# Four column tiles of 32 in place of two of 64 for the 65-column attention products of a four-layer graph-attention stack

## The chip, the core and the metric

The kernel runs on one core of a Trainium2 chip. The metric is the device time of one launch in microseconds. Before the change three runs gave 3209.97, 3210.28 and 3212.03 us; the median, 3210.28 us, is the time to compare with.

## What is computed

The input is `x` of shape (16, 1024, 256) in float32 and one adjacency matrix of 1024 x 1024 integers that all 16 batch entries share. Four graph-attention layers follow one another, each with a layer norm and a ReLU ahead of it and a residual sum behind it:

```
h = relu(layernorm(x));  x = x + L0(h, adj)     # 4 heads of 64
h = relu(layernorm(x));  x = x + L1(h, adj)     # 1 head of 256
h = relu(layernorm(x));  x = x + L2(h, adj)     # queries times keys, 1 head of 256
h = relu(layernorm(x));  x = x + L3(h, adj)     # 4 heads of 64
```

Layers 0, 1 and 3 score a pair of nodes by a leaky ReLU of (source score + target score); layer 2 scores it by a dot product. In each layer the scores are masked by the adjacency matrix, go through a softmax over the neighbours, and weigh a sum over the projected rows:

```
alpha = softmax(where(adj, leaky_relu(s_src[j] + s_dst[i]), -inf), axis=j)
h_out[i] = sum_j alpha[i, j] * Wh[j]
```

All products are in float32.

## The kernel before, in words

The function `fast` does the work; `general`, behind a flag that is found at run time, is a fallback that these inputs do not enter. All of a batch entry's rows (8 tiles of 128 nodes) stay in SBUF through the four layers, and five entries can be on the chip at a time.

The softmax is not normalised until the end. For a layer with a leaky ReLU of a sum the exponential of the score is the larger of two products of a source factor and a target factor; factors that depend on one node alone are pulled out, so that VectorE makes a whole tile of weights with one instruction at L950 (`p = max(row, ke) * mask`, 128 keys by 512 queries). TensorE then multiplies these weights with the values. The values carry one more column, which the product turns into the softmax's denominator: with heads of 64 the moving operand has 65 columns, with one head of 256 it has 257.

The order of all work is written by a planner. Every piece is a step with an engine, a cost in microseconds, a due time and the buffers that it takes and gives back (`plan.add`); `plan.order()` plays the steps through once while the program is built and gives one fixed order. Steps of different layers and different entries lie interleaved on each engine: while layer 0 of one entry runs, layer 3 of another and layers 1 and 2 of others run between its steps.

The names that matter here:

- `product` (L531 to L534) is the helper that all large products go through. It splits the 128 stationary columns into two matmuls of `COLS = 64` columns each, with outputs on PSUM partitions 0 to 63 and 64 to 127[...]. All of these matmuls have line L534.
- `steps_a` makes the weights and the products of layers 0 and 3. For each half of the queries, each head and each tile of keys there is one VectorE step `weigh` (L950) and one TensorE step `attend`: four calls of `product`, one for each 128 queries, into the tile `acc` of PSUM. One layer of one entry has 64 such steps, the kernel has 2048 of them.
- `steps_b` does the same for layers 1 and 2. Its `attend` writes the tile `accb` with 257 columns; its `score` (layer 2) writes `pp` from `qT` and `hT` with 512 columns.
- `prologue` norms and transposes a layer's input (L796: float32 transposes of 128 x 128 into `pp`) and projects it with `product` (`projected`: tiles `pp<-w,hTp` with 268 or 259 columns, `pp<-w2v,hT` with 256; `query`: `pp<-hT,w` with 512). L883 transposes the score factors, with 32 or 8 stationary columns.

A step of `steps_a` as the planner sees it on TensorE:

```
s = plan.add(PE, 0.47, at, attend, (s, last_a[1]), take=("acc",) if jt == 0 else (), give=give)
```

Of the kernel before, what the change touches and what calls it, by code (L numbers as in the profile page):

```python
# [18 lines left out]
P = 128  # L19
# [3 lines left out]
HALF = 512  # L23

COLS = 64

# [462 lines left out]
def fast(  # L491
# [35 lines left out]
    def buf(tag, shape, dtype=F32, name=None):  # L527
        pool = psum if tag in ("pp", "acc", "accb") else sb
        return pool.tile(shape, dtype, name=name or tag, tag=tag, bufs=bufs[tag])

    def product(to, stationary, moving, start, stop):  # L531

        for c in range(0, P, COLS):
            nc.tensor.matmul(  # L534
                to[c : c + COLS],
                stationary[:, c : c + COLS],
                moving,
                start=start,
                stop=stop,
                skip_group_check=True,  # L540
            )
# [17 lines left out]
    def mask_of(half, jt):  # L559
        return mask[half][jt // HT][:, jt % HT, :]  # L560
# [173 lines left out]
    class Layer:  # L734
# [5 lines left out]
        def prologue(self, due, step, stats):  # L740
# [35 lines left out]
            for n, t0 in enumerate(range(0, NT, 2)):  # L776
# [34 lines left out]
                for k in range(2):  # L811
                    t = t0 + k

                    def projected(t=t, t0=t0, k=k):
                        pv = T["pv", t] = buf("pp", [P, HALF])
                        for c in range(KC):
                            product(
                                pv[:, :cols],
                                T["hT", t0][:, c, k * P : (k + 1) * P],
                                w[:, c, :cols],  # L820
                                start=(c == 0),
                                stop=(c == KC - 1),
                            )
# [31 lines left out]
            if not self.gat:  # L855
                for dc in range(KC):
                    for n0 in range(0, N, HALF):

                        def query(dc=dc, n0=n0):
                            pq = T["pq", dc, n0] = buf("pp", [P, HALF])  # L860
                            for c in range(KC):
                                product(
                                    pq,
                                    w12[:, c, dc * P : (dc + 1) * P],
                                    self.hT[:, c, n0 : n0 + HALF],
                                    start=(c == 0),
                                    stop=(c == KC - 1),
                                )

                        s = plan.add(PE, 1.72, at, query, (*copies, *w12_ready), take=("pp",))  # L870

                        def keep(dc=dc, n0=n0):
                            nc.scalar.copy(self.qT[:, dc, n0 : n0 + HALF], T["pq", dc, n0])

                        evicted.append(plan.add(ACT, 0.6, at, keep, (s,), give=("pp",)))
                self.ready = tuple(evicted)
                return
# [61 lines left out]
    def steps_a(lay, due, span):  # L939
        heads = lay.heads  # L940
        d = F // heads
        T = {}
        n = 2 * heads * NT
        for i in range(n):
            half, hd, jt = i // (heads * NT), i // NT % heads, i % NT
            at = due + span * i / n

            def weigh(half=half, hd=hd, jt=jt):
                p = T["p", half, hd, jt] = buf("p", [P, HALF])
                nc.vector.scalar_tensor_tensor(  # L950
                    p, lay.rows[half, hd], lay.ke[:, hd, jt : jt + 1], mask_of(half, jt), op0=OP.max, op1=OP.mult
                )

            s = plan.add(
                DVE, 0.67, at, weigh, (last_a[0], *lay.ready, lay.row_ready[half, hd], *mask_ready[half, jt // HT]),
                take=("p",), give=("row4",) if jt == NT - 1 else (),
            )
            last_a[0] = s

            def attend(half=half, hd=hd, jt=jt):  # L960
                if jt == 0:
                    acc = buf("acc", [P, HALF])
                    T["acc", half, hd] = acc[:, : HT * (d + 1)].rearrange("p (t d) -> p t d", t=HT)
                p = T.pop(("p", half, hd, jt))
                for t in range(HT):
                    product(
                        T["acc", half, hd][:, t, :],
                        p[:, t * P : (t + 1) * P],
                        lay.val[:, jt, hd, :],
                        start=(jt == 0 and t == 0),  # L970
                        stop=(jt == NT - 1),
                    )

            give = ("p", "val4") if i == n - 1 else ("p",)
            s = plan.add(PE, 0.47, at, attend, (s, last_a[1]), take=("acc",) if jt == 0 else (), give=give)
            last_a[1] = s
            if jt != NT - 1:
                continue

            def divide(half=half, hd=hd):  # L980
                if hd == 0:
                    T["o", half] = buf("o", [P, HT, F])
                acc = T.pop(("acc", half, hd))
                rden = small.tile([P, HT, 1], F32, name="rden")
                nc.vector.reciprocal(rden, acc[:, :, d : d + 1])
                nc.vector.tensor_mul(  # L986
                    T["o", half][:, :, hd * d : (hd + 1) * d], acc[:, :, :d], rden.to_broadcast([P, HT, d])
                )

            s = plan.add(DVE, 0.62, at - EARLY, divide, (s,), take=("o",) if hd == 0 else (), give=("acc",))  # L990
            if hd != heads - 1:
                continue
            its = (half * HT, (half + 1) * HT)
            s = lay.elu(T, half, its, at - EARLY, (s,), (4, 2.3, 2.45), ("o",))
            if lay.layer == 3:
                b = lay.b

                def store(its=its, b=b):
                    nc.sync.dma_start(
                        out=out[b].rearrange("(t p) f -> p t f", p=P)[:, its[0] : its[1], :],  # L1000
                        in_=x_tiles[b][:, its[0] : its[1], :],
                    )

                s = plan.add(SP, 0.1, at, store, (s,))
                plan.add(LAND, 3.0, at, lambda: None, (s,), give=("x",) if half else ())
# [284 lines left out]
```

## Time and profile before

| | |
|---|---|
| median of 3 runs | 3210.28 us |
| the profiled execution, its own time | 3207.69 us |
| its span, first to last instruction | 3205.9 us |
| granted TensorE clock, mean | 0.993 |
| TensorE matmul busy | 3101.3 us, 97% |
| TensorE weight loads busy | 2150.1 us, 67% |
| VectorE busy | 2740.2 us, 85% |
| ScalarE busy | 1304.6 us, 41% |
| matmuls recorded | 48774, and as many weight loads |
| DMA | 127.41 MB, 40 GB/s on the mean |

Times of instructions are in nanoseconds or microseconds as marked. "PE" is TensorE's matmul and "PEld" its weight load, which runs beside matmuls. Matmuls are pipelined: an instruction's duration goes from its start to the modelled end of its output, and the next one starts well before that, so the sum of durations is more than the busy time, and the price of a matmul in a stream is the distance from one start to the next. A line "acc<-val,p 128*64 128x65" is a product with stationary `p` (128 rows, 64 columns), moving `val` (128 rows, 65 columns), written to `acc`.

### The profile page before, as it was taken

How to read it: one execution, taken by the hardware profiler on the slowest of the kernel's cores; microseconds unless marked ns; L12 is line 12 of the kernel's file. 1: busy time of each engine (PE TensorE's matmuls, PEld its weight loads, DVE VectorE, ACT ScalarE, POOL GpSimd, SP SyncE). 2: the span in 40 equal slices, each digit the busy share in tenths (PEclk: the TensorE clock that was granted, in tenths of full speed). 3: DMA queues.
4: the chain of work that ended last, by engine and by line, in shares of the span. 5: the costliest groups of instructions: out<-in, count | busy, mean ns of one | idle time of the engine just before them, and what ended most of it. 6: DMA issues, size and time to landing. Idle time of an engine off the chain costs nothing.

```text
span 3205.9 us, 108219 instructions
## 1 busy us (share of the span) xinstructions
PE 3101.3 (97%) x48774; PEld 2150.1 (67%) x48774; DVE 2740.2 (85%) x5584; ACT 1304.6 (41%) x3143; POOL 117.0 (4%) x89
## 2 busy tenths in 40 slices
PE   3799999999999999999999999999999999999996
PEld 2676666767676676766767676676767667675665
DVE  4987689898888989888898888989888898986697
ACT  4334444334344434434334334434434444343421
POOL 0000000000000000000000000000000000000000
PEclk9899999999999999999999999999999999999998
DMA  5101001101011010111101011110101101010011
GB/s 187 55 22 32 22 18 35 48 26 58 24 40 42 25 57 23 45 35 38 45 25 58 25 36 41 35 48 25 58 22 40 43 25 42 25 35 19 24 35 49
DMA packets 85910, 127.41 MB, mean 40 GB/s; under 512 B 8768, under 2 KB 44480, under 8 KB 85440
## 3 DMA queue, kind: packets, MB, share of 16 engines
q1 hardware_dynamic: 81408, 118.06, 11.7%
q8 instruction: 384, 6.29, 0.8%
q10 hardware_dynamic: 4032, 2.36, 0.2%
q14 instruction: 86, 0.70, 0.1%
HBM read 103.02 MB, written 17.37 MB: 38 GB/s over the span
## 4 chain that ended last, share of the span: by engine, by line
PE 92%; DVE 5%; DMA 1%; ACT 1%; issue 0%; ACTq 0%; SPq 0%
PE pp L534 31%; PE acc L534 28%; PE accb L534 27%; PE pp L796 4%; DVE p L950 3%; DMA raw<-in_adj_dram 1%; DMA w<-in_L_gnn_W_dram 0%; DVE p L1020 0%; ACT junk L1121 0%; PE pp L883 0%; DVE o L927 0%; DVE xt L928 0%; DVE bn L728 0%; DVE o L986 0%; ACT mask L656 0%
## 5 line engine op out<-in xcount | busy, mean ns | idle before, releaser
L950 DVE SCALAR_TENSOR_TENSOR p<-row,ke,mask 128x512 f32<-128x512 f32 x2048 | 1428.0, 742 | 100.3 <-PE acc L534 95.6
L534 PEld LDWEIGHTS acc<-val,p 128*64 128x64 f32 x32768 | 1073.7, 138 | 225.9 <-issue 102.6
L534 PE MATMUL acc<-val,p 128*64 128x65 f32 x32768 | 1114.0, 223 | 26.2 <-DVE p L950 26.1
L534 PE MATMUL accb<-val,p 128*64 128x257 f32 x8192 | 934.9, 380 | 0.9 <-ACT o L1085 0.9
L534 PEld LDWEIGHTS accb<-val,p 128*64 128x64 f32 x8192 | 567.2, 136 | 288.3 <-issue 6.6
L534 PE MATMUL pp<-qT,hT 128*64 128x512 f32 x2048 | 480.9, 594 | 0.0
L534 PE MATMUL pp<-w,hTp 128*64 128x268 f32 (+1 forms) x3072 | 399.1, 390 | 1.7 <-ACT hTp L807 1.7
L1047 ACT ACTIVATE u<-pp 128x512 f32<-128x512 f32 x256 | 152.8, 597 | 408.1 <-PE pp L534 361.6
L782 ACT ACTIVATE h<-xt,nshift,rstd 128x256 f32<-128x256 f32 x512 | 277.6, 595 | 80.9 <-DVE nshift L761 77.7
L534 PEld LDWEIGHTS pp<-w,hTp 128*64 128x64 f32 x3072 | 201.2, 138 | 107.7 <-issue 23.7
L534 PEld LDWEIGHTS pp<-qT,hT 128*64 128x64 f32 x2048 | 131.9, 137 | 175.0 <-issue 161.5
L728 DVE BATCH_NORM_STATS2 bn<-xt 128x6 f32<-128x256 f32 x512 | 212.3, 415 | 9.7
L756 POOL TENSOR_TENSOR rstd<-rstd,neg_half 128x8 f32<-128x8 f32 x64 | 114.5, 1789 | 2484.1 <-DVE rstd L753 2135.0
L922 ACT ACTIVATE ex<-o 128x256 f32<-128x256 f32 (+1 forms) x192 | 121.0, 630 | 206.1 <-DVE o L986 202.1
L1085 ACT ACTIVATE o<-accb,rden 128x256 f32<-128x256 f32 x128 | 60.9, 476 | 348.7 <-DVE rden L1079 348.6
L1087 ACT ACTIVATE o<-accb,rdens 128x256 f32<-128x256 f32 x128 | 60.2, 470 | 346.5 <-DVE rdens L1079 346.5
L1052 DVE SCALAR_TENSOR_TENSOR p<-u,p 128x512 f32<-128x512 f32 x256 | 174.4, 681 | 23.6 <-ACT p L1048 23.4
L1020 DVE SCALAR_TENSOR_TENSOR p<-row,ke,mask 128x512 f32<-128x512 f32 x256 | 186.1, 742 | 0.0
L1053 DVE TENSOR_TENSOR p<-p,mask 128x512 f32<-128x512 f32 x256 | 177.1, 692 | 8.8
L837 ACT ACTIVATE val<-pp 128x4 f32<-128x4 f32 (+1 forms) x384 | 67.3, 176 | 284.6 <-PE pp L534 281.4
L927 DVE SCALAR_TENSOR_TENSOR o<-ex,o 128x256 f32<-128x256 f32 (+1 forms) x192 | 131.3, 684 | 52.6 <-ACT ex L923 52.5
L796 PE MATMUL pp<-ident,h 128*128 128x128 f32 x1024 | 166.3, 289 | 9.8 <-ACT h L782 5.3
(75 smaller groups left out, 1823.6 us busy)
## 6 DMA issues: line engine op xcount, KB each, us to landing
row<-er_d SPq DMA_DIRECT2D x288, 256.0 KB, 3.2
xt<-in_x_dram SPq DMA_DIRECT2D x16, 1024.0 KB, 9.4
out_dram<-xt SPq DMA_DIRECT2D x32, 512.0 KB, 3.7
raw<-in_adj_dram SPq DMA_DIRECT2D x32, 256.0 KB, 4.5
w<-in_L_gnn_W_dram ACTq DMA_DIRECT2D x3, 256.0 KB
a_bc<-in_L_gnn_a_dram ACTq DMA_DIRECT2D x6, 128.0 KB, 9.4
wraw<-in_L_gnn_W_dram ACTq DMA_DIRECT2D x2, 256.0 KB
er_d<-er_s SPq DMA_DIRECT2D x32, 16.0 KB, 1.4
```

Source lines behind the costliest of these rows:

```text
L534: nc.tensor.matmul(to[c : c + COLS], stationary[:, c : c + COLS], moving, start=start, stop=stop, skip_group_check=True,)
L728: nc.vector.bn_stats(st, x_tiles[b][:, t, :])
L756: nc.gpsimd.tensor_tensor(T["rstd"], T["rstd"], neg_half, OP.pow)
L782: nc.scalar.activation(h, x_tiles[b][:, t, :], AF.Relu, bias=T["shift"][:, t : t + 1], scale=T["rstd"][:, t : t + 1],)
L796: nc.tensor.transpose(tp[:, c, k * P : (k + 1) * P], T["h", t0 + k][:, c * P : (c + 1) * P], ident)
L922: nc.scalar.activation(T["ex", key], T["o", key], AF.Exp)
L927: nc.vector.scalar_tensor_tensor(o, ex, -1.0, o, op0=OP.mult, op1=OP.max)
L950: nc.vector.scalar_tensor_tensor(p, lay.rows[half, hd], lay.ke[:, hd, jt : jt + 1], mask_of(half, jt), op0=OP.max, op1=OP.mult)
L1020: nc.vector.scalar_tensor_tensor(p, lay.rows[half, 0], lay.ke[:, 0, jt : jt + 1], mask_of(half, jt), op0=OP.max, op1=OP.mult)
L1047: nc.scalar.activation(u, e, AF.Exp, scale=1.0 - SLOPE)
L1052: nc.vector.scalar_tensor_tensor(p, u, 1.0, p, op0=OP.max, op1=OP.mult)
L1053: nc.vector.tensor_mul(p, p, mask_of(half, jt))
```

## The change

The helper gets a parameter for the width of a column tile, and the products of `steps_a` (layers 0 and 3) are made with 32 columns a tile. All other products keep 64.

```diff
+NARROW = 32
...
-    def product(to, stationary, moving, start, stop):
+    def product(to, stationary, moving, start, stop, cols=COLS):
 
-        for c in range(0, P, COLS):
+        for c in range(0, P, cols):
             nc.tensor.matmul(
-                to[c : c + COLS],
-                stationary[:, c : c + COLS],
+                to[c : c + cols],
+                stationary[:, c : c + cols],
                 moving,
                 start=start,
                 stop=stop,
...
                         lay.val[:, jt, hd, :],
                         start=(jt == 0 and t == 0),
                         stop=(jt == NT - 1),
+                        cols=NARROW,
                     )
```

The planner's costs, due times and buffers are as before, so every engine's steps keep their order; on TensorE each run of 65-column matmuls has twice as many of them, each with a stationary operand of 32 columns, and nothing is added, removed or moved on any other engine or queue.

## The prediction

> **What bounds the kernel now.** I read the page first: busy shares, then the chain that ended last.
>
> ```profile
> PE 3101.3 (97%) x48774; PEld 2150.1 (67%) x48774; DVE 2740.2 (85%) x5584; ACT 1304.6 (41%) x3143; POOL 117.0 (4%) x89
> PE 92%; DVE 5%; DMA 1%; ACT 1%; issue 0%; ACTq 0%; SPq 0%
> PE pp L534 31%; PE acc L534 28%; PE accb L534 27%; PE pp L796 4%; DVE p L950 3%; DMA raw<-in_adj_dram 1%; DMA w<-in_L_gnn_W_dram 0%; DVE p L1020 0%; ACT junk L1121 0%; PE pp L883 0%; DVE o L927 0%; DVE xt L928 0%; DVE bn L728 0%; DVE o L986 0%; ACT mask L656 0%
> ```
>
> TensorE's matmul queue makes 92% of the chain, and the tile that the change touches, `acc`, 28%. A busy share is a mean, so next the busy times in a stretch from the middle, where one batch entry goes in and one comes out every 190.7 us:
>
> ```profile
> 1190.70:1381.40 190.70, 190.70 (x3045) 132.63 (x3043) 169.96 (x345) 79.77 (x192) 7.34 (x5) 1.00 0.13 38
> ```
>
> The columns are length, PE, PEld, DVE, ACT, POOL, granted clock, DMA. PE is busy for all 190.70 us, DVE for 169.96. No wait is left on TensorE there that could absorb or give back anything: what a matmul costs in its stream is what the kernel costs. Last, the groups of the touched tile by form, and the timeline of PE alone (start us, length us, line, tile, count):
>
> ```profile
> L534 PE MATMUL acc<-val,p 128*64 128x65 f32 x32768 | 1114.0, 223 | 26.2 <-DVE p L950 26.1
> L534 PEld LDWEIGHTS acc<-val,p 128*64 128x64 f32 x32768 | 1073.7, 138 | 225.9 <-issue 102.6 <-DVE p L950 39.0 <-DVE o L927 7.5
> ```
>
> ```profile
> 1506.06 0.66 PE L796 MATMUL pp<-ident,h 128*128 128x128 f32 x4
> 1506.65 0.69 PE L534 MATMUL acc<-val,p 128*64 128x65 f32 x16
> 1507.16 1.07 PE L534 MATMUL pp<-w,hTp 128*64 128x268 f32 x8
> 1508.07 0.64 PE L534 MATMUL acc<-val,p 128*64 128x65 f32 x16
> 1508.53 1.05 PE L534 MATMUL pp<-w,hTp 128*64 128x259 f32 x8
> ...
> 1511.22 0.64 PE L534 MATMUL acc<-val,p 128*64 128x65 f32 x16
> 1511.79 0.66 PE L796 MATMUL pp<-ident,h 128*128 128x128 f32 x4
> ```
>
> ```profile
> 1528.29 2.97 PE L534 MATMUL acc<-val,p 128*64 128x65 f32 x96
> 1531.09 3.65 PE L534 MATMUL accb<-val,p 128*64 128x257 f32 x32
> 1534.57 2.50 PE L534 MATMUL acc<-val,p 128*64 128x65 f32 x80
> ```
>
> Take distances from start to start. 96 matmuls of 65 columns last 2.80 us (1528.29 to 1531.09): 29.2 ns each, although one has a length of 223. The two column tiles run side by side, so the unit is a pair: 48 pairs, 58.3 ns. A pair of 257 columns takes 3.48/16 = 217.5 ns; 512 columns (1484.34 to 1486.06 us, 8 matmuls) take 430. From 257 to 512 that is 0.83 ns a column. The pair is thus set by the stream of moving columns: the array is full already, and four tiles side by side stream no less than two.
>
> The second thing to see is what a change of tile width costs. Between `acc` and `pp<-w,hTp`, both 64 wide, nothing: 16 matmuls take 8 x 58.3 = 466 ns, and 1508.07 to 1508.53 is 0.46. Into the 128-wide transposes the same 16 take 0.57 (1511.22 to 1511.79), 0.10 us more. Out of them, the 16 take 0.51 (1506.65 to 1507.16), 0.05 more; and eight transposes take 1.02 (1546.30 to 1547.32) where four take 0.59, so that one is 0.108 and 0.16 is left over for going in and out. So a switch costs 0.10 us in which nothing is started, and 0.05 us in which the first weights are waited for: 0.15 us.
>
> [...]
>
> **The change part by part.** Planner and other engines keep their order; 16,384 products become 32,768, with two weight loads and two matmuls each in the records: `acc` goes from 32,768 matmuls to 65,536, in the same places.
>
> 1. The stream. 16,384 pairs (16,384 x 58.3 ns = 955 us) become 16,384 groups of four. If the four tiles run side by side, a group lasts what its moving columns last. By the line above 65 columns would be 217.5 - 192 x 0.833 = 57.6 ns; from 256 columns (`pp<-w2v,hT`, 1548.77 to 1552.32 us less 0.10 for the transposes behind: 215.6) it is 56.5. [...] I take 56.7: 16,384 x 1.6 = **-27 us**. Bounds: 0, and -43 (a slope of 0.84 ns, 55.7 ns).
> 2. New width switches. In the built program's order, `acc` follows a 64-wide product directly 525 times and is followed by one 597 times (the rest of its neighbours are transposes, where the width switched before). All 1122 cost nothing now and become switches between 64 and 32. From 32 to 64: 0.10 + 0.05, and the tiles of a group start one after the other: of a pair, two last 0.28 us together where one lasts 0.27 (the first two at 1514.91), some 7 ns apart, so the fourth starts about 13 ns later than the second did: 597 x 0.164 = **+98 us**. From 64 to 32: 0.10, and half of the 0.05, since half the columns are loaded: 525 x 0.125 = **+66 us**. The trace shows no such switch; below, 0.11 and 0.151 (+148 us together), above, 0.151 and 0.18 (+187). That a drain gives time back is excluded, since PE has no wait to save.
> 3. Switches that exist already: 188 from full width into `acc` lose about 26 ns of load, 116 out of it gain 13 ns: **-3 us**.
> 4. Instruction supply: twice as many instructions for `acc`, 64 in place of 32 a step of 467 ns. Costed at nothing[...].
> 5. VectorE's `p` and `rden` are hidden under PE in the steady stretch (169.96 of 190.70 us); a slower PE gives them more room, and may save some of the 26 us that `acc` waits for `p` (not counted, lower bound only). No queue, DMA or wait is added.
>
> Sum: -27 + 98 + 66 - 3 = +134. Against the profiled execution 3207.7 + 134 = 3341; the median of the runs shown is 2.6 us above it, so **3344 us**, own range 3300 to 3405.
>
> **The rivals.**
> - *No drain between 64 and 32: faster.* Every switch with a drain in this trace has a transpose on one side. If the drain belongs to the transpose mode and not to the tile's width, step 2 falls away and step 1 stays: 3210 - 27 - 3 = 3180, or 3210 if step 1 is nothing too. For it: the confounding; that 128 to 32 (L796 to L883) shows no drain. [...] It decides as soon as a switch costs under 24 ns (27 us / 1122).
> - *Issue becomes the bound: much slower.* A step now has 32 matmuls. [...] With today's 14.6 ns for each load or matmul it would be 64 x 14.6 = 934: +957. It decides from 7.3 ns an instruction. Against it: the two matmuls of a pair start some 7 ns apart[...]; for it: no stream in the trace goes faster than 14.6.
> - *The four tiles run two at a time:* 955 us twice, 4165. [...] I count it with the one before.
>
> **How the numbers follow.** Drain 0.62, no drain 0.22, issue or half concurrency 0.16. A measurement of this kernel tells about 0.2%, 6 us, from no change. Faster: two thirds of the no-drain case, 0.15. Same: 0.06. Slower: 0.79. The range takes the drain case and the no-drain case, 3178 to 3410; what is left out is the issue case.
>
> **What would show it.** Right: start-to-start 0.46 to 0.57 us or so for a lone step of 32 matmuls of 32 columns between 64-wide products, long runs at 57 to 58 ns a group, PE at 100% in a period of about 199 us, `accb` and `pp` rows unchanged in length but with about 0.15 us lost ahead of each. Wrong: runs of `acc` no longer than the stream between 64-wide products (no drain), or a long run of `acc` at 100 ns a group or more (issue).

## The result, and the profile after

The changed kernel takes 3445.16 us (median of 4 runs, 3443.0 to 3446.68) against 3210.12 us before: 1.0731 times as long, 95% interval 1.0712 to 1.0749, or 235 us more. The profiled execution has a span of 3442.1 us and a mean granted clock of 0.993, as before, so the clock is not the cause. Its busy shares and the chain that ended last, from the page:

```profile
PE 3250.5 (94%) x81542; PEld 2113.0 (61%) x81542; DVE 2753.6 (80%) x5584; ACT 1309.1 (38%) x3143; POOL 116.9 (3%) x89
PE 92%; issue 3%; DVE 2%; DMA 1%; ACT 1%; ACTq 0%; SPq 0%
PE pp L536 31%; PE acc L536 30%; PE accb L536 27%; PE pp L798 4%; DVE p L952 1%; DMA raw<-in_adj_dram 1%; DMA w<-in_L_gnn_W_dram 0%; ACT junk L1124 0%; PE pp L885 0%; DVE o L929 0%; DVE xt L930 0%; DVE bn L730 0%; DVE o L989 0%; ACT ex L925 0%; ACT ex L924 0%
```

The matmul count is as forecast (48774 + 32768). What is new is "issue 3%": some 100 of 3442 us, in which TensorE stood still and waited for nothing that the profile shows. Before it was 0%. A stretch of 206 us from the middle shows it too (length, PE, PEld, DVE, ACT, POOL, clock, DMA):

```profile
1412.00:1618.00 206.00, 200.89 (x5095) 130.11 (x5091) 170.70 (x344) 80.29 (x191) 7.34 (x5) 1.00 0.12 37
```

PE is busy for 200.89 of 206 us, where it was busy without a gap before. (The stretches of 206 us around it have 204.71, 204.40 and 202.04.) The group of the changed tile says the same; the last field is the idle time ahead of it and what ended it:

```profile
L536 PE MATMUL acc<-val,p 128*32 128x65 f32 x65536 | 1113.6, 222 | 103.4 <-issue 80.1 <-DVE p L952 23.0
```

The waits for VectorE's weights are the 23 us that they were. Next the timeline of PE alone, where single steps stand between 64-wide products, and one long run:

```profile
1610.02 0.66 PE L536 MATMUL acc<-val,p 128*32 128x65 f32 x32
1610.61 1.12 PE L536 MATMUL pp<-w,hTp 128*64 128x268 f32 x8
1611.66 0.66 PE L536 MATMUL acc<-val,p 128*32 128x65 f32 x32
1612.25 1.10 PE L536 MATMUL pp<-w,hTp 128*64 128x259 f32 x8
...
1633.40 2.93 PE L536 MATMUL acc<-val,p 128*32 128x65 f32 x192
1636.26 3.70 PE L536 MATMUL accb<-val,p 128*64 128x257 f32 x32
```

A lone step now takes 0.59 us from start to start, 0.46 before, and the 64-wide product behind it 1.05 (1610.61 to 1611.66), 0.91 before. That is the drain on both sides (the time that a change of width costs before the stream runs again), 0.27 us for going in and out with the faster stream already taken off. The run of 192 takes 2.86 us; less 0.14 for the two switches it is 56.7 ns a group of four: 0.14 is the sum of the parts of the two switches that fall into this distance, the wait of the first group behind the switch in (0.024) and the idle time of the switch out (0.113). And one place of another kind, in the middle of a run:

```profile
1692.71 2.36 PE L536 MATMUL acc<-val,p 128*32 128x65 f32 x152
1696.54 0.32 PE L536 MATMUL acc<-val,p 128*32 128x65 f32 x8 [1.47 <-issue]
```

After 152 matmuls TensorE stands idle for 1.47 us and then goes on, without a semaphore. Over the single instructions of this trace there are some 88 such stalls of more than 0.2 us, about 101 us in all; 23 us of them fall in the first 200 us, 57 in the middle, 22 in the last 100. Count all of TensorE's recorded instructions (loads, matmuls and its few semaphore instructions): every stall comes after 193 or 194 of them, modulo 256.

So the 235 us are: new switches +162, the stream -27, existing switches -3, stalls +101, together 233.

### The profile page after: what moved, and what is told of

It is laid out like the page before. It is cut to its first block, busy times and chain, and to the rows that moved or that the text cites. A ratio compares the mean times of both kernels' runs of the same rounds, so it can differ in the third digit from the quotient of the medians.

```text
span 3442.1 us, 173756 instructions
## 1 busy us (share of the span) xinstructions
PE 3250.5 (94%) x81542; PEld 2113.0 (61%) x81542; DVE 2753.6 (80%) x5584; ACT 1309.1 (38%) x3143; POOL 116.9 (3%) x89
## 4 chain that ended last, share of the span: by engine, by line
PE 92%; issue 3%; DVE 2%; DMA 1%; ACT 1%; ACTq 0%; SPq 0%
PE pp L536 31%; PE acc L536 30%; PE accb L536 27%; PE pp L798 4%; DVE p L952 1%; DMA raw<-in_adj_dram 1%; DMA w<-in_L_gnn_W_dram 0%; ACT junk L1124 0%; PE pp L885 0%; DVE o L929 0%; DVE xt L930 0%; DVE bn L730 0%; DVE o L989 0%; ACT ex L925 0%; ACT ex L924 0%
## 5 line engine op out<-in xcount | busy, mean ns | idle before, releaser
L536 PEld LDWEIGHTS acc<-val,p 128*32 128x32 f32 x65536 | 976.9, 110 | 433.8 <-issue 261.2
L536 PE MATMUL acc<-val,p 128*32 128x65 f32 x65536 | 1113.6, 222 | 103.4 <-issue 80.1
L536 PE MATMUL accb<-val,p 128*64 128x257 f32 x8192 | 949.0, 383 | 5.9 <-issue 5.6
L536 PE MATMUL pp<-qT,hT 128*64 128x512 f32 x2048 | 490.6, 602 | 2.4 <-issue 1.4
L536 PE MATMUL pp<-w,hTp 128*64 128x268 f32 (+1 forms) x3072 | 410.7, 397 | 3.5 <-ACT hTp L809 1.7
L1051 ACT ACTIVATE p<-pp,shift_col 128x512 f32<-128x512 f32 x256 | 174.7, 683 | 0.0
```

The source lines that it names most:

```text
L536: nc.tensor.matmul(to[c : c + cols], stationary[:, c : c + cols], moving, start=start, stop=stop, skip_group_check=True,)
L1051: nc.scalar.activation(p, e, AF.Exp, bias=shift_col, scale=SLOPE)
```

## The experiments

Each edit is shown against the changed kernel, unless another is named.

The first theory after the result: the switches cost what was forecast, and the rest is instruction supply. The page counts the DMA packets that carry instructions; those of queue 8, before and after:

```profile
q8 instruction: 384, 6.29, 0.8%
```

```profile
q8 instruction: 640, 10.49, 1.3%
```

The columns are packets, MB and share of the DMA engines. 97,548 recorded loads and matmuls before make 254 a packet, 163,084 after make 255; the 65,536 that came in addition came with exactly 256 packets more, so a packet of 16.4 KB is 256 instructions of 64 bytes. The trace also keeps the time of every single packet, and this ties the stalls to them: each of the changed kernel's 89 idle gaps of more than 20 ns that the profile puts down to issue ends between 1.22 and 1.60 us after a packet has landed, where less than 8% of all its matmuls start. The same holds for all 498 such gaps of the six runs that have any, at 1.19 to 1.61 us; the four other kernels have none. The rival: the switches upset the order of steps, and TensorE waits for VectorE's weights without the profile naming it.

**All products in tiles of 32.** No 64-wide tile is left, hence no switch between 64 and 32.

```diff
-COLS = 64
+COLS = 32
```

> All large products in tiles of 32 columns, so that no 64-wide tile is left and the 1122 new width switches are gone, while the 65-column runs need as many instructions as in the changed kernel (and the wide ones twice as many). In the changed kernel 235 us are lost: by the groups' distances, switches cost +162 and the faster stream gives -27, which leaves some 100 us that the chain of waits calls issue. Theory A, instruction supply: instructions come in blocks of 256 and not faster than one block in about 3.4 us (13.4 ns each), while a run of 32-wide 65-column groups uses one in 7.1 ns; the stalls stay or grow, since the wide products between the runs now use more too: 3210 - 27 - 15 + 100 to 180 = 3270 to 3350 us, with issue at 3% or more of the chain. Rival B, the order of steps no longer fits (waits for VectorE's weights after the switches): without switches nothing is late and the kernel is faster than before, about 3170 us.

Measured: 3392.25 us, 1.0569 (1.0552 to 1.0587). Slower than before without any new switch, so the rival falls; but above the expected range of 3270 to 3350. The chain has

```profile
PE 91%; issue 5%; DVE 2%; DMA 1%; ACT 1%; ACTq 0%; SPq 0%
```

and the single instructions show 194 stalls over 0.2 us, 191 us, nearly twice those of the changed kernel. With -27 for the stream, and -7 for earlier first matmuls after 274 transposes (27 ns each in the changed kernel), the sum is 3367; some 25 us stay unaccounted for.

**The mirror image.** The 65-column products at 64 as before, all wider ones at 32.

```diff
-COLS = 64
+COLS = 32
...
-NARROW = 32
+NARROW = 64
```

> The mirror image: the 65-column products in tiles of 64 as before, all wider ones (256 to 512 columns) in tiles of 32. As many switches between 64 and 32 as in the changed kernel (1124), but no stream that uses an instruction in under 14.6 ns. Theory A: switches alone, 526 x 0.151 + 598 x 0.125 = +154 us, 3355 to 3375 us, issue at 0% of the chain, no idle gap of a microsecond inside a run. Rival B (late VectorE work through the switches): the other 100 us appear here too, about 3465 us.

Measured: 3366.46 us, 1.0484 (1.0467 to 1.0502). As many switches as in the changed kernel, at about the forecast price (+157 us, +154 forecast); the chain has no issue in it:

```profile
PE 92%; DVE 5%; DMA 1%; ACT 1%; issue 0%; ACTq 0%; SPq 0%
```

The two kernels show each part of the change without the other: width switches without stalls cost 157 us, and narrow tiles without new switches 182. They are not the two terms of the sum: in the kernel with all products in tiles of 32 the neighbours are narrow too, and its stalls are 191 us, not 101.

**Wider products at full width.** This asks what the drain belongs to, since before the change every drain had a transpose on one side.

```diff
-COLS = 64
+COLS = 128
...
-NARROW = 32
+NARROW = 64
```

> The 65-column products in tiles of 64 as before, all wider ones at the full width of 128, one matmul a pass. No transpose stands between them, so this asks whether a switch between two plain products of different width drains, without any 32-wide tile. If the width drains: 1122 x 0.151 = +169 us, and the transposes no longer switch against the wide products (246 x 0.15 = -37 us): about 3340 us. If the drain belonged to the transposes: none between the products, 3210 us. Instruction supply plays no part (fewer instructions than before).

Measured: 3367.64 us, 1.0492 (1.0474 to 1.0509). The drain belongs to the width. The timeline of PE shows both halves of it:

```profile
1625.21 0.60 PE L798 MATMUL pp<-ident,h 128*128 128x128 f32 x4
1625.74 1.15 PE L536 MATMUL acc<-val,p 128*64 128x65 f32 x32
1626.83 0.66 PE L798 MATMUL pp<-ident,h 128*128 128x128 f32 x4
1627.41 0.69 PE L536 MATMUL acc<-val,p 128*64 128x65 f32 x16
1628.03 1.99 PE L536 MATMUL pp<-w2v,hT 128*128 128x256 f32 x8
```

16 matmuls of 65 columns between a transpose and a plain 128-wide product take 0.62 us, 0.15 more than their stream of 0.47: now the plain product drains. Four transposes behind such a product, of their own width, take 0.53 (1625.21 to 1625.74); the same four behind 64-wide ones 0.58. It came out 28 us above my 3340, and a switch into 128 costs more than I took: the first two plain 128-wide matmuls behind a switch start 0.105 us later than in their stream, not 0.05, 597 x 0.055 = 33 us.

**TensorE alone.** A kernel of nothing but runs of products, a DVE copy between the stretches. One stretch of it; `cols` is the width of a tile, `wide` the number of moving columns, and the others differ in these and in the length.

```diff
+    for k in range(320):
+        cols, wide = [(32, 65)][k % 1]
+        product(acc, k % 4, cols, wide, k == 0, k == 319, call)
```

> TensorE alone, the graph layers left out (the output is the input copied): runs of products without any wait inside, a block being all 128 stationary columns. 320 blocks of 65 columns in tiles of 64: 58.3 ns a pass, 37.3 us. The same in tiles of 32: theory A (one block of 256 instructions in 3.4 to 3.75 us) 68 to 75 us, after a start at 56.7 ns a pass out of what was fetched ahead; if only the array counted, 36.3 us. 160 blocks of 130 columns in tiles of 32: 13.9 ns an instruction, at the limit, 35.5 to 37.5 us. 80 blocks of 257 columns in tiles of 64, of 32, of 128: 34.7 us each. 80 blocks of 257 alternating 64 and 32: 79 switches x 0.14 = +11 us, 46 us; alternating 128 and 64, and 128 and 32: the same +11 us each if the width drains, nothing if only transposes do.

The timeline of PE, where no semaphore can stop a stretch:

```profile
123.35 37.55 PE L37 MATMUL a64x<-v,p 128*64 128x65 f32 x1280 [0.44 <-DVE v L46]
...
172.60 3.83 PE L37 MATMUL b32x<-v,p 128*32 128x65 f32 x254 [0.53 <-DVE v L62]
177.43 2.02 PE L37 MATMUL b32x<-v,p 128*32 128x65 f32 x128 [1.01 <-issue]
180.89 2.02 PE L37 MATMUL b32x<-v,p 128*32 128x65 f32 x128 [1.43 <-issue]
184.34 2.02 PE L37 MATMUL b32x<-v,p 128*32 128x65 f32 x128 [1.43 <-issue]
...
256.02 35.67 PE L37 MATMUL c32x<-v,p 128*32 128x130 f32 x1280 [0.53 <-DVE v L78]
292.25 34.89 PE L37 MATMUL d64x<-v,p 128*64 128x257 f32 x320 [0.55 <-DVE v L86]
...
363.09 46.27 PE L37 MATMUL f64and<-v,p 128*64 128x257 f32 x480 [0.55 <-DVE v L102]
```

Tiles of 64 go through without a stop. Tiles of 32 run for 254 matmuls and then in portions of exactly 128, that is 128 loads and 128 matmuls, 256 instructions. Each portion takes 2.02 us with its tail, and the next begins 3.45 us after the last one began (180.89 to 184.34) in 10 of 18 cases, 3.61 us on the mean of the stretch and 4.00 at the most. The stretch lasts 70 us where 36 is stream. At 13.9 ns an instruction (130 columns) nothing stops over 2560 instructions. So the supply in a long run is 256 instructions in 3.45 us at best, 13.5 ns each, and 14.1 on the mean.

The packet records say what fills these 3.45 us. A portion starts; some 1.1 us later (1.04 to 1.52) the next packet begins its transfer, which takes 0.88 to 1.38 us; and 1.24 to 1.61 us after it has landed the next portion starts. No two packets of TensorE's are under way at once, here or in any other run, and no other DMA packet is recorded in this stretch, so it is not traffic that delays them.

Stretches of 257 columns last 34.9 us in every width when it is constant; alternating 64 and 32 it is 46.3, alternating 128 with 64 or with 32 it is 48.6 and 48.1, for 79 switches 0.14, 0.17 and 0.17 us each.

**A second dose of neighbours.** If the neighbours' instructions matter, full-width neighbours should leave fewer stalls.

```diff
-COLS = 64
+COLS = 128
```

> The 65-column products in tiles of 32 as in the changed kernel, all wider ones at the full width, so that the work between the runs needs half as many instructions as in the changed kernel and a quarter of those of the all-32 kernel. Supply theory: stalls at every 256th instruction fall as the neighbours use fewer instructions: 191 us (all 32), 101 us (wide 64), here 50 to 80 us. The rest of the sum: switches into 128 cost 0.205 (seen in the kernel with wide 128) + 0.013, out of it 0.124: 597 x 0.218 + 525 x 0.124 = +195; no drain between transposes and full-width products -38; stream -27. 3210 + 130 + 65 = 3405, 3385 to 3425 us. Rival, waits for VectorE's weights: no link to the neighbours' instruction count, stalls as before at 101 us or more, since the run is longer by more switches: 3440 us or more.

Measured: 3422.61 us, 1.0651 (1.0633 to 1.0668), inside the expected range, but for its stalls, 80 with 102 us, not 50 to 80 us: here the rival's forecast came true. What speaks for the supply is that all 78 gaps put down to issue again end 1.19 to 1.61 us after a packet's landing, at the same place modulo 256; the waits for VectorE's weights are 16.8 us, less than before. With neighbours at 128 or 64 the stalls are alike (102, 101); only neighbours at 32 raise them (191). My reading is that after a 64-wide neighbour as much is read ahead as after a 128-wide one, so that halving its instructions gains nothing; no run shows what is read ahead at these places. By the sum of the terms the time should be some 20 us more; 9 of them are the shorter waits for VectorE, the rest is open.

**Half of the change.**

```diff
-                        cols=NARROW,
+                        cols=NARROW if lay.layer == 3 else COLS,
```

> Only layer 3 in tiles of 32, layer 0 at 64: half of the change. By the built program's order 517 switches between 64 and 32 (the 547 with full width stay): 517 x 0.145 = +75 us. Stream: half of the pairs, -14. Supply theory: half as many 32-wide steps, and where they alternate with layer 0's steps a block of instructions lasts longer, so stalls fall by more than half of 101 us: 20 to 45. Together 3210 + 75 - 14 + 32 = 3303, 3290 to 3320 us. If the stalls came in proportion to the switches or to the steps: 50 us, about 3321.

Measured: 3324.07 us, 1.0352 (1.0335 to 1.0369), just above the expected range. Stalls are 46 with 54 us, above the expected 20 to 45: in proportion to the narrow steps and not less, so steps of layer 0 at 64 in between gave no extra cover that shows. There are none left in the first 200 us, and as much as in the changed kernel in the last 100. The sum, 3212 + 75 - 14 + 54 = 3327, holds.

**The length of the runs.** The kernel of TensorE alone once more, with the same work cut into runs of different length. The stretch with runs of 32 blocks; the others differ in the three numbers.

```diff
+    widths = ([65] * 32 + [257] * 16) * 10
+    for k, wide in enumerate(widths):
+        product(acc, k % 4, 32, wide, k == 0, k == len(widths) - 1, call)
```

> TensorE alone again, the graph layers left out (the output is the input copied). Each stretch has 320 blocks of 65 columns and 160 of 257, all in tiles of 32, so no switch of width and the same 7680 loads and matmuls, 105.6 us of stream; only the lengths of the runs differ: 2, 16, 32, 64 or 160 blocks of 65 and then half as many of 257. Supply theory, with about two blocks of 256 instructions fetched ahead and one more each 3.45 us: runs of 2 and 16 blocks (32 and 256 instructions) are covered, 106 to 109 us; runs of 32 (512 instructions) just about, 106 to 115; runs of 64 (1024) stall twice each for 1.65 us, 122 us; runs of 160 (2560) eight times each, 132 us. With tiles of 64 and runs of 160: 107 us, no stall. If only the mean number of instructions counted, all five are alike.

Each stretch ends in a VectorE copy that waits for it, so the view of waits lists the stretches (us, times, longest), here from runs of 160 down to 2; the last line is tiles of 64:

```profile
DVE s_every L112 <- PE every L37: 141.1, 1, 141.1
DVE s_every L97 <- PE every L37: 134.9, 1, 134.9
...
DVE s_every L82 <- PE every L37: 119.4, 1, 119.4
DVE s_every L67 <- PE every L37: 111.9, 1, 111.9
DVE s_every L52 <- PE every L37: 110.7, 1, 110.7
DVE s_tiles L127 <- PE tiles L37: 107.1, 1, 107.1
```

Equal work and equal numbers of instructions, and 30 us between the shortest runs and the longest: the length of a run counts, not the mean number of instructions. The sizes were forecast too low: 110.7 and 111.9 us for runs of 2 and 16 blocks, where 106 to 109 were expected, and 119.4, 134.9 and 141.1 for 32, 64 and 160, where it was 106 to 115, 122 and 132. Tiles of 64 came out as expected. A run of 64 blocks (1024 instructions, four packets) stops three times and once more, briefly, as it ends, not twice, and one of 32 (512 instructions, two packets) stops once; the stretch of ten such runs takes 8 us more than runs of 16 (119.4 and 111.9). So less than two packets are ahead when a run begins.

**A version that beats both.** If each change of width costs 0.15 us, the kernel before has 549 of them too, most around transposes. With the transposes made eight at a time, they are 347. Against the kernel before:

```diff
+                def both(n=n):
+                    turned(2 * n)
+                    turned(2 * n + 2)
+
+                s = plan.add(PE, 1.2, at, both, tuple(before), take=("pp", "pp"), give=("h",) * 4)
...
-                s = plan.add(PE, 0.6, at, turned, (s,), take=("pp",), give=("h", "h"))
```

> The kernel before (all products 64 wide) with one thing else: the prologue's transposes, which run at full width, are made eight at a time (one planner step with two PSUM buffers) and not four, so that the order has 347 changes of width in place of 549. If a change of width costs 0.15 us wherever it stands, 202 x 0.15 = 30 us are saved: about 3180 us. Rival: the step now waits for four normed tiles and two PSUM buffers at once, and the reordered plan loses what the drains gave back: 3200 to 3230 us.

Measured: 3182.9 us, 0.991 (0.9893 to 0.9926) of the kernel before: 29 us less, as worked out from the price of the switch. The planner orders all steps anew here, so the order is a second difference; but the time is saved where the switches are, in TensorE's busy time (3070.5 us, 3101.3 before), and its idle time is about the same (108.5 us, 104.6 before). On the timeline the transposes stand in eights, 1.02 us from start to start, where two fours took 2 x 0.59:

```profile
1484.72 1.09 PE L782 MATMUL pp<-ident,h 128*128 128x128 f32 x8
1485.74 2.09 PE L534 MATMUL acc<-val,p 128*64 128x65 f32 x64
```

## Why the prediction was right and wrong

The direction was right, and so were the price and the number of the switches, which the single instructions and the other kernels confirm. The size was not: 3344 us forecast, 3445 measured, outside the range of 3178 to 3410, because a term was missing. By its steps:

- Step 1, the stream: forecast 56.7 ns a group and -27 us; the trace shows 56.7. Right. What took the other 1.6 ns of a pair before was not shown.
- Step 2, the switches: forecast 0.164 and 0.125 us, +164 together. The single instructions give 0.163 (next start 0.113 late, first pair 0.05) and 0.123 (0.099 and 0.024), +162. Right, and the mirror image, which has only this part, came out at +157. Between plain products it is the same as at the transposes: 16 matmuls of 65 columns between a transpose and a 128-wide product took 0.62 us, 0.15 more than their stream, and between two products of their own width 0.46 (1508.07 to 1508.53, before), their stream alone.
- Step 3: as forecast. Behind a transpose the first group of `acc` starts its second pass 27 ns earlier than before, and out of `acc` into transposes 12 ns are lost.
- Step 4 failed. It costed instruction supply at nothing, which was my estimate and had no reading of the trace behind it. It should have been +101 us. At these places TensorE stood idle and started the next matmuls only 1.22 to 1.60 us after a packet of instructions had landed. The cover was less than two packets of 256 instructions: the long run of TensorE alone stops after 254 loads and 254 matmuls, 508 instructions. A narrow step, 64 instructions, uses a quarter of a packet, and in that run the supply of 13.5 ns an instruction at best is slower than the 7.1 ns of the stream. The prediction priced a matmul's start, and not the bringing in of its instructions.
- The issue rival had the right cause and the wrong form. I set it beside the drain as an alternative of 957 us, as if every step would be issued slowly. It was an added term: some 88 stalls stand against 2048 steps, and in the kernel of TensorE alone a run of 508 instructions goes through before the first. In one long run the rival is close: 5120 instructions in 70 us are 0.88 us for the 64 of a step, and it said 0.934. The argument against it, that the two matmuls of a pair start some 7 ns apart, holds for what TensorE can start: four matmuls and their loads now go through in 56.7 ns, 7.1 an instruction, under the 7.3 where the rival began. Its own argument, that no stream in the trace went under 14.6 ns an instruction, was the hint that the range should have reached further up.
- The no-drain rival is refuted by the kernel with wider products at full width (the 0.15 us above, with a plain product behind). What I held for it stands in the trace before: L883 with 32 columns starts 109 ns after the last L796 in two of three places, as one L796 after another. Why these two follow each other without a drain was not tried. The four tiles run side by side, which was an assumption in the forecast: a group of four takes 56.7 ns, no longer than a pair did (58.3).
- Step 5: VectorE stayed hidden; `acc` waits 23 us for `p`, 26 before.

## What to carry to other kernels

Count changes of column width in the order of TensorE's work, and price each at what the trace shows for one that is there already; here grouping work of equal width was worth its count times that price (202 x 0.15 us, 29 measured). Where products become narrower and more numerous, put the time of one load or matmul in its stream beside the rate at which instructions arrive (here 7.1 ns beside 13.5 at best), and the length of the runs beside what is read ahead (here 508 instructions in the long run). A gap of a microsecond or so without a semaphore, at a fixed place modulo 256 of TensorE's instructions and 1.19 to 1.61 us after an instruction packet had landed, is what a lack of instructions looked like in these runs.

## What the runs showed of the hardware that I had not expected

TensorE's instructions came in packets of 256 (256 packets more for 65,536 instructions more), and no two packets were under way at once. In the long run of TensorE alone one packet takes 3.45 us or more although its own transfer takes about 1.1 us (0.88 to 1.38): the next transfer begins only some 1.1 us after the portion before it has started, and the new portion starts some 1.4 us after the landing. By my estimate from these numbers the transfer alone would keep up with the stream of 7.1 ns an instruction, which uses a packet in 1.8 us; why the one begins and the other starts so late was not tried.

A switch into the full width costs more than one into 64 or 32: in the kernel with wider products at full width about 0.205 us in and 0.14 out, where between 64 and 32 it is 0.163 into 64 and 0.123 into 32. What differs is how late the first matmuls behind the switch start: by 0.105 us for 128 columns, 0.05 for 64, 0.024 for 32. I read this as a wait for their load; where widths alternate in the kernel of TensorE alone, a load lasts 188 ns, 134 and 108. In the kernel with wider products at full width, float32 transposes behind plain 128-wide products show no drain: the first transpose starts 216 ns after the last pass of 257 columns, which is the pass itself.
